# A two-layer graph attention kernel: three of every eight layer 0 tiles gathered by indirect DMAs

## The chip, the core and the metric

The kernel runs on one core of a Trainium2 chip. The metric is the device time of one execution in microseconds (us). The engines are PE (TensorE matmuls; PEld is its weight load), DVE (VectorE), ACT (ScalarE), POOL (GpSimd) and SP, which only issues DMAs here.

## The reference

16 graphs ("batches" below) of 1024 nodes with 64 features, and an int32 adjacency matrix of 1024 x 1024 each, symmetric, with about 0.8% of its entries set and the diagonal. Two layers, each followed by a residual and a layer norm:

```
# layer 0: 8 heads of 64, edges = adj (0 or 1 here)
q, k, v = heads(x @ Wq + bq), heads(x @ Wk + bk), heads(x @ Wv + bv)
scores  = leaky_relu(q . k / 8 + edge_bias[edges], 0.2), -1e9 where edges == 0
x = layernorm(x + softmax(scores) @ v @ Wp + bp)
# layer 1: one head, additive scores
hp = x @ lin_w.T + lin_b ; u, v = hp @ W1.T, hp @ W2.T
e  = a . leaky_relu(u_i + v_j, 0.2), -9e15 where adj == 0
x  = layernorm(x + elu(softmax(e) @ hp))
```

## The kernel before, in words

**Neighbour lists.** Since a node has only about nine neighbours, the kernel never forms 1024 x 1024 scores. Eight nodes share one list of neighbour slots: `SLOTS` = 120, of which 112 hold the union of the eight nodes' neighbours and 8 the nodes themselves. `prepare` (L308) makes the lists of a batch on DVE out of the adjacency matrix (matmuls `pat` L333, then rounds of MAX8 and MATCH_REPLACE8), as columns `col` that go to DRAM and as the mask of who is whose neighbour. It is a generator of 41 pieces (`PIECES` L255). `finish` (L423) makes the mask.

**Tiles.** A batch is 8 tiles of 128 nodes, that is 16 lists. A tile of either layer passes through these methods:

- `load` (L460): a DMA on SP brings the tile's list columns to all partitions (`cb`, 544 KB).
- `indicate` (L468): two DVE instructions (L475) compare `cb` with row numbers, which gives 0/1 matrices `f`.
- `gather` (L488), in two halves `hs`: 26 bf16 matmuls each (L499) multiply the batch's features, split by `thirds` (L445, POOL) into three bf16 parts, with `f`. So the neighbours' features arrive as columns (64 features on the partitions, slots along the row); ACT copies them out of PSUM (L505) into `xg`. `own` (L481, POOL, L484) adds the 8 own columns.
- `turn` (L509): 8 transposes (L518) make rows `xn` (slots on the partitions) of `xg`, and ACT copies them out (L519).
- Layer 0: `queries`, `score` (PE L603; DVE L611, L619, L620), `exps` (ACT L629), `divide` (DVE L636, POOL L637), `turn_weights` (PE L645), `attend` (PE L655), `heads` (PE L671, every second tile), `rows`, `residual`. Layer 1: `own_rows` (POOL L728), `project` (PE L740, L746; ACT L751; DVE L752), `weigh` (PE L766), `exps`, `turn_weights` (PE L780, DVE L782), `attend`, `rows`, `residual`.

**Order.** The loop at L883 is written out by hand, and every engine executes its instructions in the order of the program (`tc.manual_schedule`). Step `g` holds tile `g` of layer 0 (the later methods belong to tiles g-1 to g-3) and tile `g - LAG` of layer 1, 12 steps behind, so that eight steps do one batch of both layers. At five places in each step `lists.place` (L858) draws pieces: those of the next batch's `prepare`, as many as `QUOTA` says, and one of a list `side` (`finish`, and layer 1's `end`). At t = 6 the next batch's `Layer0` begins (L940: transposes `px`, then `thirds` in one block on POOL), at t = 2 the batch's `Layer1`. `Norm.scale` (L547) runs on POOL over a whole batch at once.

**Buffers.** In PSUM `ps_s` has two banks, which `score`, `heads` and `project` take in turn; `ps_g`, `ps_p` two each; in `ps_z` the tag "e" is one bank, shared by `back` (the rows of both layers), `weigh`'s scores and layer 1's `turn_weights`.

Of the kernel before, what the change touches and what calls it, by code (L numbers as in the profile page):

```python
# [9 lines left out]
F32 = mybir.dt.float32  # L10
# [12 lines left out]
GR = 8  # L23
# [10 lines left out]
def kernel(  # L34
# [204 lines left out]
    root = fst.tile([P, 1], F32, name="root")  # L239
    nc.vector.memset(root, -0.5)  # L240
    setup.close()

# [11 lines left out]
    KEPT = 40  # L254
    PIECES = 41  # L255
    MULT = 4
# [24 lines left out]

    started, edges, masks, late = {}, {}, {}, {}

    def start(b):

        xs = dbl.tile([P, NT, D], F32, tag="xs", bufs=3, name=f"xs_{b}")
        dg = sml.tile([P, NT], I32, tag="dg", bufs=2, name=f"dg_{b}")
        diag = adj[b].rearrange("r c -> (r c)")[0 : N * N : N + 1]
        for n in range(2):
            nc.sync.dma_start(xs[sub(n), :, :], by_rows(x[b], n))  # L290
            nc.sync.dma_start(
                dg[sub(n), :], diag[n * 512 : n * 512 + 512].rearrange("(t r) -> r t", r=D)
            )
        ads = {}

        def load(k):
            hs, T = divmod(k, NT)
            if hs < 2:
                ads[k] = dbl.tile([P, 2, SEG], I32, tag="ad", bufs=4, name=f"ad_{b}_{hs}_{T}")
                nc.sync.dma_start(  # L300
                    ads[k], adj[b, ts(T, P), :].rearrange("p (n c) -> p n c", n=2)[:, :, hs * SEG : hs * SEG + SEG]
                )

        for k in range(4):
            load(k)
        started[b] = xs, dg, ads, load

    def prepare(b):  # L308

        if b not in started:  # L310
            start(b)
        xs, dg, ads, load = started.pop(b)
        flags = sml.tile([P, 32], F32, tag="flags", bufs=2, name=f"flags_{b}")
# [95 lines left out]
        yield  # L409

        rows_s = per.tile([P, NT, 2 * CAP2], BF16, tag="rows_s", name=f"rows_s_{b}")
        for n in range(2):
            for q in range(NQ):
# [5 lines left out]
                )  # L419
        edges[b] = (xs, col_d)  # L420
        late[b] = (flags, dg, rows_s)

    def finish(b):  # L423

        flags, dg, rows_s = late.pop(b)
        mask = dbl.tile([P, NT, SLOTS], BF16, tag="mask", bufs=4, name=f"mask_{b}")
        nc.vector.tensor_scalar(mask[:, :, 0 : 2 * CAP2], rows_s, code, NEG, ALU.not_equal, ALU.mult)
# [17 lines left out]
    def thirds(src, tag, nm):  # L445

        t3 = dbl.tile([P, 3, NT, D], BF16, tag=tag, bufs=3, name=f"{tag}_{nm}")
        rest = src
        less = per.tile([P, NT, D], F32, tag="less", name=f"less_{tag}_{nm}")
        for k in range(3):  # L450
            nc.gpsimd.tensor_copy(t3[:, k, :, :], rest)
            if k < 2:
                nc.gpsimd.tensor_tensor(less, rest, t3[:, k, :, :], ALU.subtract)
                rest = less
        return t3

    class Tiles:


        def load(self, t):  # L460
            nm = f"{self.b}_{self.layer}_{t}"
            self.cb[t] = cb = dbl.tile([P, NSEG, 2, NQ, WIN], BF16, tag="cb", bufs=3, name=f"cb_{nm}")
            nc.sync.dma_start(
                cb.rearrange("p s n q k -> p (s n q k)"),
                self.col_d[t].rearrange("s n q k -> (s n q k)").unsqueeze(0).to_broadcast([P, NSEG * 2 * NQ * WIN]),
            )
# [54 lines left out]
        def begin(self, x_):  # L521

            b = self.b
            px = ps_g.tile([P, 512], F32, tag="g", name=f"px{self.layer}_{b}")
            columns_T(px, x_)
            self.xT = dbl.tile([P, 512], F32, tag=f"xT{self.layer}", name=f"xT{self.layer}_{b}")
            nc.scalar.copy(self.xT, px)
            self.t3 = thirds(x_, "x3", f"{self.layer}_{b}")
            self.f, self.xg, self.xn = {}, {}, {}

    def banks(tag, name):
# [3 lines left out]
    class Norm:  # L535
# [10 lines left out]

        def scale(self, dst, y):  # L547
            rs = sml.tile([P, NT], F32, tag="rs", name=f"rs_{self.nm}")
            nc.gpsimd.tensor_tensor(rs, self.mv[:, :, 1], eps.to_broadcast([P, NT]), ALU.add)
            nc.gpsimd.tensor_tensor(rs, rs, root.to_broadcast([P, NT]), ALU.pow)  # L550
            nc.gpsimd.tensor_tensor(dst, y, self.mv[:, :, 0:1].to_broadcast([P, NT, D]), ALU.subtract)
            nc.gpsimd.tensor_tensor(dst, dst, rs.unsqueeze(2).to_broadcast([P, NT, D]), ALU.mult)  # L552

    class Layer0(Tiles):
        layer = 0

        def __init__(self, b):
            self.b, self.cb, (self.xs, self.col_d) = b, {}, edges[b]
            self.begin(self.xs)
            self.mx = dbl.tile([P, 2, NG // 4], F32, tag="mx", name=f"mx_{b}")  # L560
            self.y = dbl.tile([P, NT, D], F32, tag="y", name=f"y0_{b}")
            self.norm = Norm(f"0_{b}")
            self.qp, self.ls, self.den, self.w = {}, {}, {}, {}

        def constants(self):
# [124 lines left out]
        def residual(self, t):  # L690
            if t % 2 == 0:
                return
            nc.vector.tensor_tensor(self.y[:, t - 1 : t + 1, :], self.pr, self.xs[:, t - 1 : t + 1, :], ALU.add)
            for t_ in (t - 1, t):
                self.norm.look(self.y, t_)

        def end(self):
            x1 = dbl.tile([P, NT, D], F32, tag="x1", name=f"x1_{self.b}")
            self.norm.scale(x1, self.y)

# [3 lines left out]
            nc.vector.tensor_tensor(bad, bad, low, ALU.max)  # L704
            return x1

    class Layer1(Tiles):
        layer = 1

        def __init__(self, b, x1):  # L710
            self.b, self.cb, self.x1, (_, self.col_d) = b, {}, x1, edges[b]
            self.begin(x1)
# [4 lines left out]
        def sums(self):  # L717
            pu = ps_g.tile([P, NT, D], F32, tag="g", name=f"pu_{self.b}")
            for t in range(NT):
                for n in range(2):  # L720
                    nc.tensor.matmul(pu[sub(n), t, :], self.xT[:, ts(t, D)], w1h[:, n, :], start=True, stop=True)
            self.u = dbl.tile([P, NT, D], F32, tag="u", name=f"u_{self.b}")
            nc.vector.tensor_tensor(self.u, pu, rows_b[:, 0:1, :].to_broadcast([P, NT, D]), ALU.add)
# [85 lines left out]
        def end(self):  # L809
# [12 lines left out]
            norm = Norm(f"1_{b}")  # L822
            for t in range(0, NT, 2):
                norm.look(y, t)
                norm.look(y, t + 1)
                yield
            norm.scale(o, y)
            yield
            for n in range(2):
# [7 lines left out]
    PLACES = 5  # L837
    QUOTA = (3, 3, 5, 6, 6, 6, 6, 6)
    l0, l1 = {}, {}
# [6 lines left out]
    class Lists:  # L846


        def __init__(self):
# [6 lines left out]
            self.done, self.part, self.side = 0, None, []  # L856

        def place(self, g, k):  # L858
            b, t = divmod(g + AHEAD, NT)
            due = PIECES * b + sum(QUOTA[:t]) + QUOTA[t] * (k + 1) // PLACES  # L860
            last = k == PLACES - 1
            while self.done < due and self.part != ("keys" if last else "sums"):
                self.part = next(self.work, None)
                self.done += 1
# [7 lines left out]
    with tc.manual_schedule(engines={getattr(mybir.EngineType, e) for e in order}):  # L872
        for _ in prepare(0):
            pass
        for _ in finish(0):
            pass
        l0[0] = Layer0(0)
        l0[0].constants()
        l0[0].load(0)
# [3 lines left out]
        for g in range(NT * B + LAG + 7):  # L883
            u = g - LAG
            b, t = divmod(g, NT)
            if t == 0 and 0 < b < B:
                lists.side.append(finish(b))
            lists.place(g, 0)
            at(l0, g - 2, "exps", 0, range(4))
            at(l0, g - 1, "score", lambda: at(l0, g - 2, "divide", 0))  # L890
            if (g - 1) // NT not in l0:
                at(l0, g - 2, "divide", 0)
            at(l0, g - 2, "exps", 1, range(2))
            at(l0, g, "gather", 0)
            at(l0, g - 3, "heads")
            at(l0, g, "gather", 1)
            at(l0, g - 2, "exps", 1, range(2, 4))
            back = ps_z.tile([P, 3, D], F32, tag="e", name=f"back_{g}") if g > 3 else None
            at(l1, u - 3, "rows", back)
            at(l0, g - 3, "rows", back)  # L900
            at(l0, g, "queries")
            at(l1, u - 3, "residual")
            at(l0, g - 3, "residual")
            if t == 6 and b - 2 in l1:
                lists.side.append(l1[b - 2].end())
            at(l0, g - 2, "divide", 1)
            at(l1, u - 1, "project")
            lists.place(g, 1)
            at(l1, u, "gather", 0)
            at(l0, g - 1, "turn")  # L910
            lists.place(g, 2)
            at(l1, u - 1, "weigh")
            at(l1, u - 1, "exps")
            at(l0, g + 1, "indicate")
            at(l0, g + 2, "load")
            at(l1, u, "gather", 1)
            if t == 2 and b - 1 in l0:
                x1 = l0[b - 1].end()
            at(l0, g - 2, "turn_weights")
            at(l1, u - 2, "turn_weights")  # L920
            at(l1, u - 1, "turn")
# [15 lines left out]
            if t == 3 and b - 1 in l1:  # L937
                l1[b - 1].sums()
            if t == NT - AHEAD and b + 1 < B:
                l0[b + 1] = Layer0(b + 1)  # L940
                l0[b + 1].load(0)
# [415 lines left out]
```

## Time and profile before

| | us |
|---|---|
| three runs, median | 2505.18 (2500.58 to 2507.12) |
| the profiled execution | 2508.74 |
| its span in the trace | 2506.8 |
| PE, DVE, ACT, POOL busy in it | 2308.1, 2012.1, 1445.2, 912.9 |
| first score of layer 0 (L603) | at 102.3 |
| eight steps of the middle (1366.9 to 1512.1) | 145.2 |
| last score of layer 0 | at 2354.1 |

The page of a profile gives busy times over the whole span. For a kernel of repeated steps the windows view is of more use: it cuts the trace at the start of each step's score and gives each engine's busy time between the cuts. The waits view says who waited for whom, and the timeline shows instructions in order. A window in the tables below is one step of the loop; t is its number in the batch, 0 to 7.

### The profile page before, as it was taken

The numbers are of one execution on the slowest core, as the hardware profiler recorded it, in microseconds if no ns is written. First come the engines' busy times: TensorE is split into PE (matmuls) and PEld (weight loads), VectorE is DVE, ScalarE is ACT, GpSimd is POOL, SyncE is SP. The second block draws the span as 40 slices with busy tenths as digits, with TensorE's granted clock in tenths as the row PEclk, the third lists the DMA queues.
The fourth block names the chain that finished last, engine by engine and source line by source line (L and its number), as shares of the span: only waits on it lengthen the run. The fifth ranks groups of instructions, "written<-read, shape, count | busy, mean of one in ns | idle before, by whom it ended". The sixth has DMA issues, their size and how long they took to land. (4 is left out here: it accounts for less than half of the span.)

```text
span 2506.8 us, 110853 instructions
## 1 busy us (share of the span) xinstructions
PE 2308.1 (92%) x48706; PEld 1957.7 (78%) x48706; DVE 2012.1 (80%) x5237; ACT 1445.2 (58%) x4401; POOL 912.9 (36%) x1106
## 2 busy tenths in 40 slices
PE   5387999999999999999999999999999999999986
PEld 3376788878788887878788787888878888888864
DVE  6687879888888988888898888889888888876642
ACT  0154656656565665656566566656656665666743
POOL 1133333434334343433434343342434434243331
PEclk9998999999999999999999999999999999999998
DMA  3412332423233242323324232332423233221210
GB/s 102 122 59 89 104 103 78 133 77 116 73 102 108 78 133 80 114 73 107 103 78 133 84 109 75 106 103 78 133 86 108 81 100 106 62 92 57 66 52 18
DMA packets 190543, 230.66 MB, mean 92 GB/s; under 512 B 91492, under 2 KB 157092, under 8 KB 190052
## 3 DMA queue, kind: packets, MB, share of 16 engines
q1 hardware_dynamic: 190052, 223.49, 28.3%
q8 instruction: 384, 6.29, 1.0%
q14 instruction: 107, 0.88, 0.1%
HBM read 218.23 MB, written 5.21 MB: 89 GB/s over the span
## 5 line engine op out<-in xcount | busy, mean ns | idle before, releaser
L499 PE MATMUL pg<-f,x 128*64 128x272 bf16 (+2 forms) x13312 | 804.5, 272 | 37.4 <-DVE f L475 34.5
L499 PEld LDWEIGHTS <-x 128*64 128x64 bf16 x13312 | 662.0, 109 | 115.5 <-issue 70.4
L637 POOL TENSOR_TENSOR ls<-ls,den 128x480 f32<-128x480 f32 x256 | 285.8, 1117 | 921.1 <-DVE den L636 912.6
L475 DVE TENSOR_SCALAR f<-cb,jrow 128x2176 bf16<-128x2176 bf16 x512 | 491.6, 1001 | 0.3 <-DMA cb<-col_d 0.3
L505 ACT COPY xg<-pg 128x448 f32<-128x448 f32 x512 | 271.5, 530 | 356.1 <-PE pg L499 355.1
L629 ACT ACTIVATE ls<-ls,mx 128x120 f32<-128x120 f32 x1024 | 391.2, 386 | 4.8 <-DVE mx L620 4.8
L519 ACT COPY xn<-pt 120x512 f32<-120x512 f32 x512 | 277.3, 597 | 11.8 <-PE pt L518 7.1
L751 ACT ACTIVATE r<-pz 128x480 f32<-128x480 f32 x256 | 132.1, 568 | 247.0 <-PE pz L746 247.0
L518 PE MATMUL pt<-ident,xg 128*120 128x128 f32 x2048 | 273.9, 276 | 0.0
L484 POOL COPY xg<-xT 128x64 f32<-128x64 f32 x256 | 107.2, 426 | 387.9 <-PE pt L518 345.4
L518 PEld LDWEIGHTS pt<-ident,xg 128*120 128x120 f32 x2048 | 224.0, 137 | 27.3 <-issue 24.8
L752 DVE SCALAR_TENSOR_TENSOR r<-pz,r 128x480 f32<-128x480 f32 x256 | 155.4, 649 | 50.6 <-ACT r L751 50.6
L629 ACT ACTIVATION_READ_ACCUMULATOR ls<-ls,mx 128x1 f32 x1024 | 194.8, 190 | 0.0
L619 DVE SCALAR_TENSOR_TENSOR ls<-sc 128x480 f32<-128x480 f32 x256 | 191.5, 748 | 0.0
L620 DVE TENSOR_REDUCE mx<-ls 128x4 f32<-128x480 f32 x256 | 167.2, 653 | 8.8
L611 DVE TENSOR_TENSOR sc<-s,rowc 128x480 f32<-128x480 f32 x256 | 155.1, 647 | 22.7 <-PE s L603 21.0
L746 PEld LDWEIGHTS pz<-rw,ub 64*64 64x64 f32 x4096 | 122.6, 133 | 63.9 <-issue 58.5
L655 PE MATMUL z<-w,xn 120*64 120x64 f32 x4096 | 159.2, 227 | 4.4 <-ACT w L647 4.4
L587 DVE TENSOR_TENSOR qp<-pq,qb 128x512 f32<-128x512 f32 x128 | 87.9, 686 | 90.0 <-PE pq L586 89.8
L655 PEld LDWEIGHTS z<-w,xn 120*64 120x64 f32 x4096 | 138.4, 139 | 27.7 <-ACT w L647 19.4
L645 PE MATMUL pp<-ident,ls 128*120 128x128 f32 x1024 | 142.0, 280 | 19.3 <-POOL ls L637 16.6
L740 PE MATMUL pz<-xg,w2d 64*64 64x480 f32 x1024 | 140.4, 588 | 17.1 <-DVE sc L611 17.1
(212 smaller groups left out, 3881.1 us busy)
## 6 DMA issues: line engine op xcount, KB each, us to landing
cb<-col_d SPq DMA_DIRECT2D x256, 544.0 KB
ad<-in_adj_dram SPq DMA_DIRECT2D x256, 256.0 KB
xs<-in_x_dram SPq DMA_DIRECT2D x32, 128.0 KB
rows_s<-slot_d SPq DMA_DIRECT2D x256, 14.0 KB
out_dram<-o SPq DMA_DIRECT2D x32, 128.0 KB
col_d<-col SPq DMA_DIRECT2D x128, 4.2 KB
dg<-in_adj_dram SPq DMA_DIRECT2D x32, 2.0 KB
slot_d<-slot SPq DMA_DIRECT2D x16, 28.0 KB
```

What stands on the lines that cost most here:

```text
L475: nc.vector.tensor_scalar(fj.rearrange("p s n q k -> p (s n q k)"), cb.rearrange("p s n q k -> p (s n q k)"), jrow[:, j : j + 1], None, AL ...
L499: nc.tensor.matmul(pg[sub(n), :, FIRST * a_ + lo : FIRST * a_ + to], self.t3[:, k, 4 * hs + 2 * a_ + j, :], f[j][:, 2 * hs + a_, n, :, lo:to],
L505: nc.scalar.copy(dst, pg)
L518: nc.tensor.transpose(pt[:, q, :], xg[:, 4 * m + q, :], ident)
L519: nc.scalar.copy(self.xn[t][:, ts(m, 4), :], pt)
L611: nc.vector.tensor_tensor(sc, both[n], self.rowc[:, n, ts_].unsqueeze(2).to_broadcast([P, 4, SLOTS]), ALU.add)
L619: nc.vector.scalar_tensor_tensor(ls, scs[n], SLOPE, scs[n], ALU.mult, ALU.max)
L620: nc.vector.tensor_reduce(self.mx[:, n, ts_], ls, XX, ALU.max, negate=True)
L629: nc.scalar.activation(ls[:, q, :], ls[:, q, :], AF.Exp, bias=neg[:, q : q + 1], accum_out=den[:, q : q + 1])
L637: nc.gpsimd.tensor_tensor(ls, ls, den.unsqueeze(2).to_broadcast([P, 4, SLOTS]), ALU.mult)
L655: nc.tensor.matmul(zz[sub(n), q, :], xn[:, q, sub(n)], w_[n][:, q // 2, sub(q % 2)], start=True, stop=True)
L752: nc.vector.scalar_tensor_tensor(r, pz[n], SLOPE / (1.0 - SLOPE), r, ALU.mult, ALU.add)
```

## The change

- `start` also copies the batch's `x` into a DRAM `table` of 1025 rows, of which row 0 is a filler (three DMAs on SP). `prepare` makes, beside `col`, the 120 row numbers of every list (`tb`, `at_s`: six DVE instructions), one PE transpose and one DVE instruction bring them to `at_d` (lists along the row, slots on the partitions). It has 43 pieces now.
- `FETCHED = (2, 5, 7)`: for these layer 0 tiles `load`, `indicate` and `own` do nothing. `fetch` issues, from POOL, one indirect DMA for each of a tile's 16 lists: 120 rows of 64 f32, straight into the layout of `xn`. `Lists.fetches` spreads the 48 of a batch over the 40 places of eight steps, ahead of the other work of a place, two steps ahead of the tile that is being worked on. `gather` of such a tile is 8 transposes of `xn` into `xg` with two ACT copies; `turn` does nothing.
- In a fetched tile's step the order is another: both halves of the gather first, `queries` ahead of `heads`, and `turn` of the tile before earlier.
- Layer 1's `turn_weights` goes from behind `weigh` and the second half of layer 1's gather to a place ahead of them.
- `place` draws at most two pieces (except at the last place of a round of eight steps). `thirds` becomes five pieces on the side list; the next batch's `Layer0` begins at t = 4 and not 6. `Norm.scale` works on two tiles at a time, in place in layer 0. `u` and layer 1's `xT` have one buffer and not two, `mask` three and not four.

```diff
-    PIECES = 41
+    PIECES = 43
...
+            nc.sync.dma_start(
+                table[1 : N + 1, :].rearrange("(t n r) d -> n t r d", n=2, r=D)[n],
+                x[b, n * 512 : n * 512 + 512, :].rearrange("(t r) d -> t r d", r=D),
+            )
...
+    def fetch(b, t, k):
+        _, table, rows_at = edges[b]
+        if k == 0:
+            fetched[b, t] = dbl.tile([SLOTS, NQ, P], F32, tag="xf", bufs=3, name=f"xf_{b}_{t}")
+        n, q = divmod(k, NQ)
+        g = D * n + NQ * t + q
+        nc.gpsimd.indirect_dma_start(
+            out=fetched[b, t][:, q, sub(n)], out_offset=None, in_=table[:, :],
+            in_offset=bass.IndirectOffsetOnAxis(ap=rows_at[:, g : g + 1], axis=0),
+        )
...
+        def gather(self, t, hs):
+            if t not in FETCHED:
+                return super().gather(t, hs)
...
+            for q in range(4):
+                nc.tensor.transpose(pt[:, q, :], self.xn[t][:, 4 * hs + q, :], ident[0:SLOTS, 0:SLOTS])
+            nc.scalar.copy(self.xg[t][:, ts(hs, 4), :], pt)
...
-    QUOTA = (3, 3, 5, 6, 6, 6, 6, 6)
+    QUOTA = (3, 3, 5, 6, 6, 6, 7, 7)
+    FETCHED = (2, 5, 7)
...
+            end = self.done + 2 if (t, k) != (NT - 1, PLACES - 1) else due
...
+            if t in FETCHED:
+                at(l0, g, "gather", 0)
+                at(l0, g, "gather", 1)
+                at(l0, g - 2, "exps", 1, range(2))
+                at(l1, u - 3, "rows", back)
+                at(l0, g, "queries")
+                at(l0, g - 3, "heads")
...
             at(l1, u, "gather", 0)
-            at(l0, g - 1, "turn")
+            at(l1, u - 2, "turn_weights")
+            if t not in FETCHED:
+                at(l0, g - 1, "turn")
...
             at(l0, g - 2, "turn_weights")
-            at(l1, u - 2, "turn_weights")
             at(l1, u - 1, "turn")
```

## The prediction, written before the changed kernel was run

> **What bounds the kernel now.** I read the page first, then the windows of one batch, then the timeline of a step, then who waited for whom. The page's first line:
>
> ```profile
> PE 2308.1 (92%) x48706; PEld 1957.7 (78%) x48706; DVE 2012.1 (80%) x5237; ACT 1445.2 (58%) x4401; POOL 912.9 (36%) x1106
> ```
>
> PE leads and DVE is near, but an average over the span does not say which of them ends a step. The windows, cut at each step's score (t = 0 to 7), do. Columns: length, then busy us of PE, PEld, DVE, ACT, POOL with counts, granted clock, DMA share, GB/s.
>
> ```profile
> 1366.90:1384.30 17.40, 17.40 (x347) 14.41 (x346) 12.24 (x26) 12.56 (x43) 6.31 (x9) 1.00 0.56 183
> 1384.30:1404.80 20.50, 18.81 (x414) 16.06 (x413) 18.01 (x51) 9.79 (x28) 10.42 (x12) 1.00 0.09 32
> 1404.80:1423.90 19.10, 17.45 (x374) 15.05 (x373) 18.64 (x45) 12.00 (x39) 6.00 (x8) 1.00 0.24 70
> 1423.90:1442.30 18.40, 17.67 (x381) 14.86 (x379) 15.88 (x43) 10.57 (x31) 3.77 (x5) 1.00 0.41 126
> 1442.30:1457.90 15.60, 15.60 (x344) 13.73 (x341) 13.31 (x32) 10.87 (x33) 3.84 (x5) 1.00 0.13 39
> 1457.90:1475.80 17.90, 17.90 (x415) 15.60 (x413) 14.51 (x36) 12.02 (x37) 5.32 (x6) 1.00 0.29 74
> 1475.80:1494.50 18.70, 18.48 (x411) 15.37 (x409) 17.08 (x44) 12.59 (x43) 16.34 (x20) 1.00 0.60 201
> 1494.50:1512.10 17.60, 17.45 (x378) 14.87 (x377) 15.14 (x42) 9.58 (x27) 4.58 (x5) 1.00 0.21 66
> sum 145.20, PE 140.75 PEld 119.94 DVE 124.80 ACT 89.99 POOL 56.59; mean PE 17.59 PEld 14.99 DVE 15.60 ACT 11.25 POOL 7.07
> ```
>
> Steps 0, 4 and 5 are PE from end to end. PE is idle for 4.5 us a batch, nearly all at t = 1 to 3, where DVE is at its fullest. The waits of PE in these 145.2 us agree; all of the larger ones are DVE's:
>
> ```profile
> PE po L671 <- DVE sc L611: 1.5, 2, 1.0
> PE pz L740 <- DVE sc L611: 0.8, 1, 0.8
> PE e L766 <- DVE r L752: 0.7, 2, 0.5
> ```
>
> So PE sets the end of a batch, DVE is behind it with 86% of the time, and POOL has 88.6 us to spare.
>
> **What goes from PE.** The timeline at t = 0 (start, duration):
>
> ```profile
> 1368.12 2.99 PE L499 MATMUL pg<-f,x 128*64 128x272 bf16 x52
> 1370.93 0.28 PE L280 MATMUL back<-lin,aT 128*64 128x64 f32 x4
> ...
> 1379.56 1.04 PE L518 MATMUL pt<-ident,xg 128*120 128x128 f32 x8
> 1380.52 1.15 PE L655 MATMUL z<-w,xn 120*64 120x64 f32 x32
> ```
>
> From its start to the next group's start a layer 0 gather holds PE for 2.81 us, a `turn` for 0.96 us. A fetched tile loses both and gains eight transposes of `xn`, which have 120 columns and not 128, so at most the same 0.96. That is 3 x 2.81 = 8.4 us less per batch; the transpose for `at_d` adds the 0.11 us from L780's start (1379.45) to the next. Net 8.3 of 145.2, and 136.9 if PE's idle time stayed at 4.5.
>
> **DVE.** Six `indicate` instructions fewer at 1.0 us (L475's mean on the page) are -6.0. Added per batch: six small ones on 128 x 136 or fewer elements and one of 120 x 128. The like rows are 0.30 (L393), 0.23 (L390), 0.17 (L401 to L403) and 0.29 (L782): about 1.7 us. Net -4.3, or 120.5. It is ill placed, though: the indicates go at t = 1, 4 and 6 (one step ahead of their tile), PE's gathers at t = 2, 5 and 7. At t = 2 DVE still has its 18.6 us, against 17.45 - 2.8 = 14.6 on PE. That tile's gain will largely turn into waiting for DVE. In return t = 1 (DVE 18.0 in 20.5) gets air, and two pieces per place at most keep long runs of list work from standing ahead of a score in DVE's queue. I take PE's idle time as 6.0 in place of 4.5; from 2.5 (the cap and the earlier layer 1 transpose end half the waits) to 10.5 (t = 2 and t = 0 wholly DVE's) are the ends.
>
> **POOL.** No row shows an indirect DMA. Nearest rows: 0.43 us for L484's copy of 128 x 64, as many values as a fetch brings; 1.12 and 1.14 for the half-row products; 1.86 for the slowest, the power:
>
> ```profile
> L637 POOL TENSOR_TENSOR ls<-ls,den 128x480 f32<-128x480 f32 x256 | 285.8, 1117 | 921.1 <-DVE den L636 912.6
> L484 POOL COPY xg<-xT 128x64 f32<-128x64 f32 x256 | 107.2, 426 | 387.9 <-PE pt L518 345.4
> ```
>
> Ends 0.43 and 1.86; I take 1.15, their middle and L637's size. 48 fetches are 20.6, **55.2** or 89.3 us per batch. `Norm.scale` in pairs is 8 x (0.2 + a power of two columns, by a quarter of 1.86 about 0.47, + two of 128 columns at about 0.45) = 12.6 for 2 x 4.4 before, +3.8; three own copies fewer, -1.2. POOL comes to 56.6 + 2.6 + 55.2 = 114 of some 138. In front of every `divide` (L637) there now stands a fetch or two. Their cover is the time from `divide` to `turn_weights`, some 6 us of project, gather, turn and weigh at t = 0. A backlog of four fetches would use it up. The thirds' block at t = 6, which made POOL 16.3 of 18.7, is spread out; unspread it would not fit beside six fetches (6.9 us) there.
>
> [...]
>
> **The rest.** ACT: four copies of 0.53 to 0.60 go and two of that size come per tile, on an engine with 55 us free. SP: three `cb` issues fewer, three for `table` more; DMA's share is 0.60 at most. `px` (1.05 us on PE) moves from t = 6 to t = 4. The first fetch of a batch waits for `at_d`; behind it on POOL stands tile 4's `divide`. One buffer for `u` makes DVE's L723 at t = 3 wait for POOL's last L728 of the batch before; behind it stand the next places' list pieces and, a step on, the scores. It costs what POOL is late, 0 to 1 us, and lies in the 6.0. At the start 12 fetches (13.8 us) and then `thirds` (4.2) follow `at_d`, which can't be there before DVE ends the lists at 76.7. So the first gather comes near 96 and not at 93.6: +3. In the tail the last normalisation is shorter by some 3. They cancel.
>
> **The sum.** 145.2 - 8.3 + 1.5 = 138.4 a batch, 6.8 less. Fifteen batches run this way (344.7 us onwards at full width, the second nearly so): -102. In the first batch, whose eight steps take 103.5 us with PE far from full, six indicates less save 3 and seven new instructions take 1 to 2: nothing. The profiled execution of 2508.7 (span 2506.8) becomes 2407; it lay 3.6 above the median of the runs, so against that median the forecast is **2403**. With 2.5 or 10.5 of idle time it is 2350 or 2470.
>
> **Rivals.**
> - *DVE takes the place of PE.* POOL goes from 39% to about 83% busy, so more of the 26 remaining indicates run beside it. If all took 1.37 us like the pair at 1405, DVE would gain 26 x 0.37 = 9.6 and stand at 130; at t = 2 and 0 nothing would hide it. I price it at 5 us a batch: 2478. For it: L475 from 772 to 1798 ns. Against it: those two ran beside products of 512 columns, and no row shows an indirect DMA beside L475.
> - *POOL becomes the bound, slower than before.* POOL needs 59.2 + 48 c. It passes my 138.4 at c = 1.65 and today's 145.2 at c = 1.79 us per fetch. At the upper end, 1.86, a batch is 148.5: +3.3 x 15 and some 5 at the start, 2560. For it: the row of 1.86 for only 8 columns. Against it: all other rows with as many values are far below.
> - *It doesn't do what it says.* The order within the fetched steps turns the freed 2.8 us into waits of PE for ACT's copies of `xg` behind four exps: no change, 2505. Against it: PE has queries and rows (1.3 us) in between.
>
> **Chances.** Forecast 0.60 (its own range 2350 to 2470), DVE 0.12, POOL 0.21, no change 0.05, other 0.02. Faster by over 0.3% (about what a measurement of this kernel can tell from no change) 0.72, within it 0.05, slower 0.23. The range 2350 to 2560 leaves out some 0.07 below and 0.10 above.
>
> **What would show it.** L499 down to 10,816 matmuls and near 650 us; windows of 15 to 16 us at t = 5 and 7 and hardly shorter ones at t = 2; fetches near 1.15 us on POOL, and POOL near 114 of 138. I am wrong if POOL is full in every window, if PE waits for `pp` on POOL's `ls`, if L475's mean passes 1.2 us, or if PE's idle time per batch is over 12 us.

## The result, and the profile after

The changed kernel takes **2906.8 us** (median of 4 runs, 2900.1 to 2924.0) against 2504.8 before: 1.162 times the time, 95% interval 1.160 to 1.164. The forecast was 2403, and 2350 to 2560 the range. It is slower by 402 us, and no rival had a price near that.

The page of the changed kernel (span 2902.4 us). First the engines' busy time, then the granted clock of PE in 40 slices, then two groups: the fetch and the indicator rows:

```profile
PE 2454.6 (85%) x46226; PEld 1999.0 (69%) x46226; DVE 1980.5 (68%) x5261; ACT 1395.4 (48%) x4305; POOL 1760.5 (61%) x2213
...
PEclk9877889999989989999999999999998889989998
...
L615 POOL DMA_INDIRECT xf<-table,at_d x768 | 815.9, 1062 | 220.9 <-issue 180.7
...
L519 DVE TENSOR_SCALAR f<-cb,jrow 128x2176 bf16<-128x2176 bf16 x416 | 383.4, 963 | 0.0
```

PE has 2480 matmuls fewer and is yet busy for 146 us more. POOL, from which the fetches were expected to take most, is at 61% and is not the bound. A fetch costs it 1.06 us, and 0.24 us of idle time stand ahead of each (180.7 us over some 740 of them).

The windows of one batch in the middle, cut at each step's score (t = 0 to 7), in the columns of the table before:

```profile
1603.50:1623.60 20.10, 18.22 (x349) 14.89 (x348) 12.44 (x24) 10.73 (x33) 15.35 (x19) 1.00 0.62 189
1623.60:1646.90 23.30, 18.79 (x368) 15.05 (x368) 19.89 (x64) 11.70 (x36) 13.84 (x17) 1.00 0.18 47
1646.90:1664.70 17.80, 17.62 (x362) 15.11 (x361) 13.63 (x31) 10.86 (x36) 10.36 (x11) 0.90 0.54 141
1664.70:1691.20 26.50, 22.26 (x411) 18.59 (x409) 17.34 (x48) 10.76 (x33) 16.34 (x20) 0.88 0.15 37
1691.20:1710.00 18.80, 15.02 (x297) 12.49 (x297) 16.32 (x36) 10.93 (x33) 12.40 (x14) 0.95 0.09 12
1710.00:1730.40 20.40, 19.11 (x373) 16.09 (x372) 13.62 (x32) 11.01 (x34) 11.11 (x15) 0.86 0.39 103
1730.40:1753.40 23.00, 19.80 (x366) 14.77 (x365) 13.24 (x37) 13.19 (x46) 20.41 (x30) 0.93 0.56 176
1753.40:1772.70 19.30, 16.87 (x370) 14.30 (x370) 16.27 (x46) 7.81 (x20) 10.35 (x15) 1.00 0.05 10
sum 169.20, PE 147.68 PEld 121.27 DVE 122.74 ACT 86.99 POOL 110.17; mean PE 18.46 PEld 15.16 DVE 15.34 ACT 10.87 POOL 13.77
```

A batch takes 169.2 us, 24 more than before. PE is idle for 21.5 of them (169.20 - 147.68), not for 4.5. It is also busy for 147.7 and not for the 132.5 that three gathers fewer should leave. The clock column says a part of why: it was 1.00 in all eight windows before, and falls to between 0.86 and 0.95 in five of them now. DVE (122.7) and POOL (110.2) are where the prediction put them (120.5 and 114). So the amount of work on these two engines is not the loss; PE itself has become slow.

What PE waited for, over the whole run:

```profile
PE z L752 <- ACT w L744: 67.3, 109, 2.2
PE pi L457 <- DVE at_s L443: 45.9, 13, 22.6
PE e L860 <- DVE eT L876: 45.6, 65, 1.9
PE px L290 <- issue: 31.6, 93, 0.5
PE prc L669 <- issue: 30.7, 53, 2.5
...
PE s L700 <- issue: 24.9, 61, 1.3
```

Three of the six say "issue": PE waited for nothing that the profile shows. Summed over all lines, such idle time of over 60 ns is 124 us here and was 5 us before. No wait of this kind stood in the prediction, so the experiments look for its cause.

### The profile page after: what moved, and what is told of

It reads as the page before. It is cut to its first block, busy times and chain, and to the rows that moved or that the text cites. A ratio compares the mean times of both kernels' runs of the same rounds, so it can differ in the third digit from the quotient of the medians.

```text
span 2902.4 us, 106586 instructions
## 1 busy us (share of the span) xinstructions
PE 2454.6 (85%) x46226; PEld 1999.0 (69%) x46226; DVE 1980.5 (68%) x5261; ACT 1395.4 (48%) x4305; POOL 1760.5 (61%) x2213
## 4 chain that ended last, share of the span: by engine, by line
PE 65%; DVE 21%; issue 5%; ACT 5%; another core or an unknown queue 1%; DMA 1%; POOL 1%; SPq 0%; POOLq 0%; ACTq 0%; DVEq 0%
PE pg L543 15%; PE s L700 7%; PE pt L562 6%; DVE f L519 4%; PE pq L683 4%; PE z L752 4%; PE pz L834 4%; PE pp L742 4%; PE pa L885 4%; PE pz L840 3%; DVE r L846 3%; PE e L860 3%; PE po L768 3%; PE pat L356 3%; PE px L290 2%
## 5 line engine op out<-in xcount | busy, mean ns | idle before, releaser
L615 POOL DMA_INDIRECT xf<-table,at_d x768 | 815.9, 1062 | 220.9 <-issue 180.7
L543 PE MATMUL pg<-f,x 128*64 128x272 bf16 (+2 forms) x10816 | 698.6, 281 | 9.7 <-issue 7.2
L543 PEld LDWEIGHTS <-x 128*64 128x64 bf16 x10816 | 558.5, 113 | 96.8 <-issue 54.6
L549 ACT COPY xg<-pg 128x448 f32<-128x448 f32 x416 | 220.9, 532 | 500.0 <-PE pg L543 396.5
L519 DVE TENSOR_SCALAR f<-cb,jrow 128x2176 bf16<-128x2176 bf16 x416 | 383.4, 963 | 0.0
L562 PE MATMUL pt<-ident,xg 128*120 128x128 f32 x1664 | 225.7, 277 | 27.0 <-ACT xg L549 26.7
L563 ACT COPY xn<-pt 120x512 f32<-120x512 f32 x416 | 226.3, 601 | 39.1 <-PE pt L562 34.5
L562 PEld LDWEIGHTS pt<-ident,xg 128*120 128x120 f32 x1664 | 185.5, 139 | 39.9 <-ACT xg L549 31.8
L752 PEld LDWEIGHTS z<-w,xn 120*64 120x64 f32 x2560 | 99.5, 142 | 111.7 <-ACT w L744 87.4
L885 PE MATMUL pa<-eT,xn 120*64 120x8 f32 x4096 | 162.1, 209 | 4.1 <-ACT xn L563 2.8
```

Of the source, the lines that this page charges most:

```text
L519: nc.vector.tensor_scalar(fj.rearrange("p s n q k -> p (s n q k)"), cb.rearrange("p s n q k -> p (s n q k)"), jrow[:, j : j + 1], None, AL ...
L543: nc.tensor.matmul(pg[sub(n), :, FIRST * a_ + lo : FIRST * a_ + to], self.t3[:, k, 4 * hs + 2 * a_ + j, :], f[j][:, 2 * hs + a_, n, :, lo:to],
L549: nc.scalar.copy(dst, pg)
L562: nc.tensor.transpose(pt[:, q, :], xg[:, 4 * m + q, :], ident)
L563: nc.scalar.copy(self.xn[t][:, ts(m, 4), :], pt)
L615: nc.gpsimd.indirect_dma_start(out=fetched[b, t][:, q, sub(n)], out_offset=None, in_=table[:, :], in_offset=bass.IndirectOffsetOnAxis(ap=r ...
```

## The experiments

**A. Which part of the change costs the time.** Three kernels take the change apart. The first has all the edits but no fetched tile:

```diff
-    FETCHED = (2, 5, 7)
+    FETCHED = ()
```

> The changed kernel with an empty list of fetched tiles: no indirect DMA, every layer 0 tile gathered by matmuls in the old order; the capped pieces, the spread thirds, the pairwise normalisation, the early layer 1 transpose and the row numbers' transpose stay. Theory A (the indirect DMAs on POOL cost the time, through waits of PE and the clock that falls after them): about the time before, 2480 to 2530 us, and few 'issue' gaps on PE. Theory B (the order around the fetches - the early layer 1 transpose, the pieces, less matmul work between dependent steps - costs it): well above, 2600 us or more.

Measured: 2528.1 us, 1.010 [1.007, 1.013] times the kernel before. All that the change does besides fetching (the list of rows, the table, the capped pieces, `Norm.scale` in pairs, the thirds in pieces, the early transpose) costs 25 us by itself.

The second issues all 768 fetches and uses none of them (every tile is gathered by PE, in the old order):

```diff
+    USED = ()
...
-            if t not in FETCHED:
+            if t not in USED:
```

> All 768 indirect DMAs are issued as in the changed kernel, but nothing reads what they bring: every layer 0 tile is gathered by matmuls in the old order. Theory A: 2750 us or more, with the 'issue' gaps of PE in px and prc and half-clock stretches as in the changed kernel. Theory B: within 60 us of the kernel without fetched tiles.

Measured: 2924.1 us, 1.168 [1.161, 1.175]. **The fetches alone add 396 us**, though nobody waits for one. The idle time of PE on issue is 136 us.

The third is the reverse: the order and the savings of the change, but no DMA. The fetched tiles are a tile of zeros that lies ready:

```diff
-        nc.gpsimd.indirect_dma_start(
...
+            fetched[b, t] = still
```

> The changed kernel with its order and its transposes of fetched tiles, but without the indirect DMAs: the fetched tiles are read from one constant tile of zeros, so the neighbours' features of tiles 2, 5 and 7 are left out of the computation. Theory A: what the prediction's sum gives, 2380 to 2420 us. Theory B: 2800 us or more, because the waits for eT, w and xg remain without any DMA.

Measured: 2462.5 us, 0.984 [0.981, 0.987]. Even fetches that cost nothing would have brought 41 us and not 102. In a batch in its middle, cut at the scores as before, PE's work is what was forecast (shown are t = 2, 3 and 7 and the sum):

```profile
1390.10:1406.20 16.10, 15.79 (x366) 13.87 (x365) 15.69 (x41) 10.82 (x37) 8.47 (x9) 1.00 0.60 167
1406.20:1426.70 20.50, 18.47 (x414) 15.81 (x413) 16.80 (x48) 10.67 (x32) 5.68 (x9) 1.00 0.10 34
...
1476.80:1495.20 18.40, 16.61 (x374) 14.09 (x373) 15.85 (x46) 8.63 (x25) 8.05 (x14) 1.00 0.07 21
sum 140.70, PE 132.66 PEld 111.87 DVE 117.85 ACT 86.56 POOL 62.80; mean PE 16.58 PEld 13.98 DVE 14.73 ACT 10.82 POOL 7.85
```

PE is busy 8.1 us less than before (140.75), against a forecast of 8.3, and idle for 8.0 us, against a forecast of 6.0 within 2.5 to 10.5. The steps are not the ones that were forecast: t = 2, which was to be hardly shorter, falls from 19.1 to 16.1 us, while t = 3 grows from 18.4 to 20.5 and t = 7 from 17.6 to 18.4. Over the third to the fifteenth batch the gain is 4.0 us each (141.7 for 145.7). The start gives some of it back: the first score comes at 107.5 us for 102.3, and the first two batches take 252 us for 242.

The early transpose was tried by itself, put back behind the second half of the gather in the changed kernel:

```diff
-            at(l1, u - 2, "turn_weights")
             at(l0, g + 1, "indicate")
...
             at(l0, g - 2, "turn_weights")
+            at(l1, u - 2, "turn_weights")
```

> The changed kernel with layer 1's transpose of its weights back behind layer 0's, as before; all else as changed. If the early transpose costs what PE waits for eT before the scores (45.6 us in the trace) and half as much again by the clock: 2830 to 2860 us. If it is of no account: 2890 to 2920 us.

Measured: 2805.9 us, 1.121 [1.114, 1.127], so the early place costs about 101 us in the changed kernel. The same edit in the kernel without DMAs and in the one without fetched tiles:

> The free fetch (no DMA; the fetched tiles are read from a tile of zeros, so the output is not the reference's) with layer 1's transpose of its weights back in its old place behind the gather. Free fetches with the early transpose gave 2462.5 us, 41 under the kernel before, where the gathers taken away are worth 102. Theory 1: PE waits at the early transposes for the second exps and for w (z from ACT w 41 us there) and moving them back gives most of the missing 61: 2405 to 2430 us. Theory 2: the order is not to blame, the remaining 61 are other edits (Norm in pairs, thirds in pieces, the turn behind queries) and the clock: 2450 to 2475 us.

> No tile fetched, all other edits in, but layer 1's transpose of its weights back in its old place. With it early, the same kernel took 2528.1, 25 over the kernel before. Theory 1 (the early transpose costs by itself): 2500 to 2510 us. Theory 2 (the 25 us are the other edits, the list of rows, the table, Norm in pairs): 2520 to 2530 us.

Measured: 2493.0 us (0.996 [0.994, 0.998]) and 2508.8 us (1.002 [1.001, 1.003]). With free fetches the early place is better by 30 us, a sign that neither theory of the first text had. Without fetched tiles it is worse by 19, and that is most of the 25 us above (theory 1 of the second text). So the early transpose isn't good or bad by itself; what decides it is not shown by these runs.

**B. What it is about a fetch.** All kernels from here on are the second one (fetches issued, nothing used; 2924 us), with the instruction replaced; they stand against the 2528 us without fetches. First POOL's time without a DMA, a memset of about a fetch's length:

```diff
-        nc.gpsimd.indirect_dma_start(
...
+        nc.gpsimd.memset(idle, 0.0)
```

> The kernel whose fetches nobody reads (2924 us; without fetches 2528), with a memset of 128 x 1120 f32 on POOL (about 1.04 us by the setup's row of 0.95 us for 1024) in the place of each of the 768 indirect DMAs: POOL is as busy, no DMA. If what costs is that POOL's own products stand behind the fetches: 2850 us or more. If it is the DMAs: 2520 to 2600 us, without 'issue' gaps of PE at the score.

Measured: 2800.8 us, 1.118 [1.112, 1.124], so +273. By the time alone, two thirds of the loss would be POOL's occupancy. The pages contradict that; the kernel with memsets, then the one with fetches:

```profile
L614 POOL MEMSET idle<- 128x1120 f32 x768 | 882.2, 1149 | 19.6
...
L519 DVE TENSOR_SCALAR f<-cb,jrow 128x2176 bf16<-128x2176 bf16 x512 | 582.6, 1181 | 0.5 <-DMA cb<-col_d 0.5
```

```profile
L615 POOL DMA_INDIRECT xf<-table,at_d x768 | 818.1, 1065 | 207.5 <-issue 182.1
...
L519 DVE TENSOR_SCALAR f<-cb,jrow 128x2176 bf16<-128x2176 bf16 x512 | 438.3, 899 | 8.1 <-PE pt L562 7.3
```

The memsets lengthen DVE's indicator rows to 1.18 us (0.85 without fetches), DVE is busy for 2300 us, and half the chain that ended last is DVE's. PE's idle time on issue is 4 us. The memset makes a loss of its own, by DVE; it doesn't stand for the full fetch, which leaves the row at 0.90 and DVE busy for 2012 us. The experiment was ill chosen.

Then the same bytes without POOL, and with POOL (`nc.gpsimd.dma_start`) but without indices:

```diff
-        nc.gpsimd.indirect_dma_start(
...
+        nc.sync.dma_start(fetched[b, t][:, q, sub(n)], table[8 * g : 8 * g + SLOTS, :] if g < 100 else table[0:SLOTS, :])
```

> The same kernel with 768 plain DMAs of the same 120 rows of 256 bytes from the table, issued on SP in place of POOL's indirect ones. If the traffic of small rows costs: 2850 us or more. If the issuing on POOL costs: 2530 to 2620 us (some 0.5 us of SP's queue each, 23 us of a batch, ahead of the cb loads).

> The same kernel with 768 plain DMAs of 120 rows of 256 bytes issued on POOL: the same bytes by POOL's queue, without the list of row numbers. If a DMA's issue on POOL costs whatever it fetches: 2850 us or more. If only the indirect form does: under 2650 us.

Measured: 2534.6 us (1.012 [1.006, 1.017]) from SP, +7, and 2575.5 us (1.028 [1.021, 1.035]) from POOL, +47. The traffic is as good as free, though these DMAs read 120 consecutive rows and not scattered ones. A plain DMA holds POOL for 0.62 us.

Then the size of an indirect fetch, by its rows and by the length of a row:

```diff
-            out=fetched[b, t][:, q, sub(n)], out_offset=None, in_=table[:, :],
-            in_offset=bass.IndirectOffsetOnAxis(ap=rows_at[:, g : g + 1], axis=0),
+            out=fetched[b, t][0:16, q, sub(n)], out_offset=None, in_=table[:, :],
+            in_offset=bass.IndirectOffsetOnAxis(ap=rows_at[0:16, g : g + 1], axis=0),
```

> The same kernel with indirect DMAs of 16 rows in place of 120. If the cost goes with the number of DMAs: 2800 us or more. If it goes with the rows: the extra time over 2528 is a seventh, about 2580 us. POOL's instruction: near 1.06 us still if its time is fixed, near 0.3 us if it goes by rows.

> The fetches issued and not used, with 64 rows each in place of 120 (the kernel without fetches 2528; 16 rows 2613; 120 rows 2924). POOL's time for one should stay near 1.0 us, as with 16 rows (0.96) and 120 rows (1.06). Theory 1: PE's instructions are held up while the descriptors of an indirect DMA are made, by the row: a line through 16 and 120 rows gives 2757 us (2700 to 2810), and PE's idle time put down to issue, 2.6 us with 16 rows and 136 with 120, lies near 65. Theory 2: it is POOL's occupancy alone: as with 16 rows, 2600 to 2640. Theory 3: something overflows between 64 and 120 rows: also near 2613, or near 2924 if it overflows below 64.

> The fetches issued and not used, 96 rows of 256 bytes each (16 rows 2613 us, 64 rows 2611, 120 rows 2924; 120 rows of 32 bytes 2633). If the holding up of PE grows with the bytes beyond those of 64 rows, a line from 64 to 120 rows gives 2790 (2720 to 2850), with 70 to 100 us of PE idle on issue; if it is a limit that only 120 rows exceed, 2600 to 2640; if a limit between 64 and 96 rows sets it, 2880 to 2940.

The same edit with 64 and with 96. For shorter rows the table is read as rows of 8 or 32 values:

```diff
-            out=fetched[b, t][:, q, sub(n)], out_offset=None, in_=table[:, :],
+            out=fetched[b, t][:, q, D * n : D * n + 8], out_offset=None,
+            in_=table.rearrange("r (a d) -> (r a) d", d=8),
```

> The fetches issued and not used, 120 rows each but of 32 bytes in place of 256, so that the bytes are those of the 16-row kernel (2613 us) and the number of indices that of the 120-row one (2924). Theory 1: the number of indices counts: 2890 to 2950 us, and PE idle on issue 110 to 160 us. Theory 2: the bytes count: 2600 to 2640 us, and issue under 10 us.

> The fetches issued and not used, 120 rows of 128 bytes each, so 15 KB, about the bytes of 64 rows of 256 (2611 us), with the indices of the full fetch (2924). If the bytes of one fetch decide, 2610 to 2650 us and issue under 20 us; if the number of rows decides once they are longer than 32 bytes, 2850 to 2940; if both count by a product, between, about 2750.

| rows x bytes | KB | us | over 2528 | POOL us each | PE idle on issue, us |
|---|---|---|---|---|---|
| 16 x 256 | 4 | 2613.3 | 85 | 0.96 | 3 |
| 64 x 256 | 16 | 2611.5 | 83 | 1.01 | 19 |
| 96 x 256 | 24 | 2609.9 | 82 | 1.03 | 18 |
| 120 x 32 | 4 | 2633.5 | 105 | 1.07 | 7 |
| 120 x 128 | 15 | 2639.3 | 111 | 1.07 | 9 |
| 120 x 256 | 30 | 2924.1 | 396 | 1.06 | 136 |

(The last row is the second kernel of part A. POOL's times are the means on the pages.) This refutes a price per row, per byte or per us of POOL for the large step: POOL's time hardly changes. The smaller fetches cost 82 to 111 us (the plain DMAs of POOL 47). On top of it, only the full fetch makes PE slow, by about 290 us more. With rows of 256 bytes there is a jump between 24 KB (82 us) and 30 KB (396 us), not a slope.

Two things come with the 82 to 111 us: POOL is held for a microsecond 768 times, and DVE's own instructions last longer. The engines and one group of DVE without fetches, then with 96 rows:

```profile
PE 2308.7 (91%) x48722; PEld 1957.1 (77%) x48722; DVE 1973.3 (78%) x5357; ACT 1447.6 (57%) x4401; POOL 1015.2 (40%) x1493
...
L716 DVE SCALAR_TENSOR_TENSOR ls<-sc 128x480 f32<-128x480 f32 x256 | 175.6, 686 | 0.0
```

```profile
PE 2336.3 (90%) x48722; PEld 1973.4 (76%) x48722; DVE 2063.1 (79%) x5357; ACT 1446.9 (56%) x4401; POOL 1750.8 (67%) x2261
...
L716 DVE SCALAR_TENSOR_TENSOR ls<-sc 128x480 f32<-128x480 f32 x256 | 207.4, 810 | 0.0
```

The same 5357 instructions of DVE take 90 us more here, and 88 to 107 us more with the other four small fetches. It is 62 us with the plain DMAs of POOL. What PE loses, it may lose to POOL's lateness or to DVE's, and no run separates the two. The large step is not DVE's: with full fetches DVE is busy for only 39 us more than without fetches.

The waits of PE with full fetches, then with 96 rows (the only entry on issue among its largest):

```profile
PE s L700 <- issue: 55.9, 160, 0.5
...
PE prc L669 <- issue: 20.7, 37, 3.4
PE pg L543 <- issue: 18.1, 59, 1.0
```

```profile
PE pi L457 <- issue: 10.7, 11, 1.0
```

How such a stretch looks. In the kernel with full fetches, three windows within a step, in the columns of the windows above:

```profile
1318.60:1320.60 2.00, 2.00 (x72) 1.93 (x70) 1.97 (x3) 1.70 (x9) 1.81 (x2) 1.00 0.94 277
1320.60:1322.85 2.25, 1.13 (x17) 0.46 (x6) 1.31 (x5) 1.21 (x7) 1.94 (x3) 1.00 0.59 127
1322.85:1323.10 0.25, 0.24 (x8) 0.24 (x12) 0.06 (x1) 0.00 (x0) 0.10 (x1) 1.00 0.82 171
```

And its timeline there (start, duration, idle time before in brackets):

```profile
1319.73 1.30 POOL L615 DMA_INDIRECT xf<-table,at_d  x1 [0.19 <-issue]
1320.19 0.82 PE L700 MATMUL s<-xg,qp 64*64 64x120 f32 x17
...
1321.31 0.36 PE L700 MATMUL s<-xg,qp 64*64 64x120 f32 x2 [0.31 <-issue]
1321.34 0.99 POOL L615 DMA_INDIRECT xf<-table,at_d  x1 [0.30 <-issue]
...
1322.10 0.36 PE L700 MATMUL s<-xg,qp 64*64 64x120 f32 x2 [0.43 <-issue]
...
1322.86 0.38 PE L700 MATMUL s<-xg,qp 64*64 64x120 f32 x4 [0.40 <-issue]
```

The 48 matmuls of a score depend on nothing that is late: 18 of them have run in 0.82 us (the line counts 17, since its window begins at 1320.50). Then PE starts two at 1321.31, two at 1322.10 and the next at 1322.86, waiting for nothing that the profile shows in between, at full clock. Two fetches stand on POOL in this stretch, and neither ACT nor DVE has idle time put down to issue in it. Over the whole run, 133 of the 136 us of such idle time end within 1.8 us of the start of a fetch, which is 42% of the run. PE's instructions coming late would be another cause, but the loads of the queue that the profile calls "instruction" are the same 384 and take no longer (1.08 us on average, 1.10 without fetches).

Since the second kernel runs the same 48,722 matmuls in the same order as the one without fetches, the time from each start to the next can be subtracted. PE's run is 386 us longer by that. **312 of them lie between the start of a fetch on POOL and 0.6 us after its end**, a part of the time that is 40% of the run. With 96 rows the same sum is 59 of 75, so it is the amount that differs and not the share. Against 16 rows the lines that lose most are the score (131 us), the turn (43), the gather (40), `prc` (30) and `px` (28): mostly groups of short f32 matmuls, of which PE starts many per us (18 in 0.82 us of the score above).

**C. Whether that is the loss of the changed kernel.** The changed kernel's order, tiles of zeros as in the third kernel, and fetches that nobody reads: first with rows of 32 bytes, then the full ones:

```diff
             fetched[b, t] = still
+            xf[b, t] = dbl.tile([SLOTS, NQ, P], F32, tag="xf", bufs=2, name=f"xf_{b}_{t}")
+        nc.gpsimd.indirect_dma_start(
...
```

> The changed kernel with fetches of 120 rows of 32 bytes, which hold POOL as long (1.07 us) and PE hardly, and with the fetched tiles read from a tile of zeros (the output is not the reference's). Without any DMA this order took 2462. If POOL's occupancy adds here what it added in the old order (2633 - 2528 = 105): 2567 (2540 to 2590). If the new order is more exposed to POOL's lateness than the old one: 2620 to 2700.

> The changed kernel, with all its fetches of 120 rows of 256 bytes issued, but the fetched tiles read from a tile of zeros (the output is not the reference's), so that no transpose waits for a transfer. With rows of 32 bytes it took 2593, 314 less than the changed kernel. If the loss lies in the issue and the size of the fetches: 2870 to 2910 us. If PE's waiting for the fetched rows has a part in it, lower by that part, at most the 23 us by which 314 exceeds the 291 of the old order.

Measured: 2593.1 us (1.035 [1.031, 1.040]) and 2884.0 us (1.152 [1.149, 1.156]). With the third kernel and the changed one this is a chain in which, from the second row on, each link changes one thing (the last link also gives the fetched tiles three buffers and not two):

| | us | step |
|---|---|---|
| before | 2504.8 | |
| changed order, fetches free | 2462.5 | -42 |
| + fetches of 120 x 32 bytes | 2593.1 | +131 |
| + rows of 256 bytes: PE slow to issue | 2884.0 | +291 |
| + the transposes read what was fetched | 2906.8 | +23 |

(The -42 is against the median of all runs of before; the 41 above is against those taken with that kernel.) The +291 is what the old order showed (396 less 105). The +131 is a little more than the 105 of the old order; here too DVE is busy for longer, 2003.4 us for 1907.6 in the kernel with free fetches. A batch of the kernel with narrow fetches, its steps t = 3 to 5 and its sum:

```profile
1483.80:1506.00 22.20, 20.19 (x417) 17.16 (x413) 17.30 (x45) 10.77 (x33) 15.21 (x20) 0.92 0.14 34
1506.00:1525.10 19.10, 16.24 (x300) 13.69 (x298) 17.48 (x36) 11.92 (x39) 15.13 (x17) 0.88 0.09 8
1525.10:1543.90 18.80, 18.80 (x370) 15.98 (x370) 13.06 (x32) 9.87 (x30) 9.47 (x12) 0.85 0.36 97
...
sum 151.30, PE 138.97 PEld 116.97 DVE 123.43 ACT 86.68 POOL 109.14; mean PE 17.37 PEld 14.62 DVE 15.43 ACT 10.83 POOL 13.64
```

Against free fetches (140.70, PE 132.66) PE is idle for 4.3 us more, and busy for 6.3 us more with the same matmuls. With them comes a lower granted clock: 0.92, 0.88 and 0.85 in the three steps shown, 1.00 in all of them with free fetches. As an estimate from these three shares and the lengths of the steps, 6.9 us at full clock are lacking, which covers the 6.3. So the smaller fetches are paid twice, as a wait and as a slower PE. The clock records of the kernels before and after have two values alone, 1.00 and 0.50 (half clock below). In the trace with narrow fetches more idle time stands ahead of half clock than elsewhere: of the 8 us ahead of a half-clock stretch, PE was idle for 2.5 on average (39 stretches, the first 110 us left out), and for 0.8 of any 8 us. Over the whole run PE is at half clock for 64 us before, 132 with free fetches, 267 with narrow ones, 421 with full ones (the kernel of 2884.0 us) and 458 in the changed kernel.

The old place of layer 1's transpose in this kernel:

> As the kernel with fetches of 32-byte rows and tiles of zeros, but with layer 1's transpose of its weights back in its old place. Without DMAs the old place is worse by 30 us (2493 against 2462), with the full fetches it is better by 100 (2806 against 2907). If POOL's lateness by occupancy makes the early transposes wait (the weights pass POOL's divide), the old place is better here too: 20 to 80 us under the kernel with the early one. If only PE's being held up does, it stays worse by about 30.

Measured: 2608.0 us (1.041 [1.034, 1.048]), 15 us over the early place. By the two intervals that can be told neither from nothing nor from 30, but a gain of 20 to 80 is excluded: what the smaller fetches do to POOL and DVE isn't what makes the early transpose a loss. It is worse by 101 us only with the full fetches, where PE is slow to issue. By which wait that comes about was not separated.

Last, a mend that computes the same values: a fetch takes only the 112 rows of the lists (28 KB), and the 8 own rows, which lie one behind the other, come by a plain DMA:

```diff
+        if q == 0:
+            first = n * 512 + t * D
+            nc.sync.dma_start(
+                fetched[b, t][2 * CAP2 : SLOTS, :, sub(n)],
+                x[b, first : first + D, :].rearrange("(q j) d -> j q d", j=GR),
+            )
...
-            in_offset=bass.IndirectOffsetOnAxis(ap=rows_at[:, g : g + 1], axis=0),
+            in_offset=bass.IndirectOffsetOnAxis(ap=rows_at[0 : 2 * CAP2, g : g + 1], axis=0),
```

> The changed kernel with the rows of each fetch cut from 120 to the 112 of the lists; the 8 own rows of each group, which lie one behind the other, come by one plain DMA of SP for 8 groups. The fetches of 96 rows of 256 bytes cost 82 us over the kernel without them, those of 120 rows 396. If the limit lies above 112 rows, PE's idle time on issue falls from 124 us to under 25 and the time to that of the kernel with narrow fetches (2593) plus the 192 plain DMAs: 2590 to 2650. If it lies between 96 and 112, the time stays at 2880 to 2920.

Measured: 2883.4 us (1.152 [1.146, 1.158]), PE idle on issue 133 us. 112 rows of 256 bytes show the large step too; with 96 rows, in the old order (2609.9 us, 18 us on issue), it was not there. The 23 us gained are no cure.

No version with fetches that was tried beats the kernel before: even fetches of 120 x 32 bytes, with 7 us of idle time on issue in part B, cost 131 us, where the changed order with free fetches brings 42.

## Why the prediction was wrong, step by step

**The step that failed is the price of a fetch.** The prediction counted a fetch as POOL's own time, free to the kernel short of "a backlog of four fetches", and put its effect on PE at nothing. With POOL's time as forecast, the runs show +131 us for the smaller fetches and +291 us more for 120 rows of 256 bytes, with which PE becomes slow to issue.

**PE's saving was right.** 8.3 us per batch forecast, 8.1 measured with free fetches. The gathers' matmuls are 10,816, as said. They were put near 650 us; they take 665.0 with free fetches and 698.6 in the changed kernel, where PE issues slowly (124 us idle on issue) and is at half clock for longer (458 us for 132).

**DVE's sum was right, its rows were not.** 120.5 us forecast, 117.9 with free fetches, 123.4 with narrow ones and 122.7 after. The rival "DVE takes the place of PE" looked at the indicator rows. Its 1.37 us are half of this line of the timeline before, a pair that ran beside POOL's work for `thirds`; the row's median in that batch was 0.78 us:

```profile
1405.08 2.73 DVE L475 TENSOR_SCALAR f<-cb,jrow 128x2176 bf16<-128x2176 bf16 x2
```

Over the run the rows' mean went down, from 1.00 to 0.96 us (0.85 without fetches). But the smaller fetches lengthen other rows (part B), so a part of that rival came; how large a part of the 131 us stays open. On POOL a fetch takes 0.98 to 1.47 us, median 1.02.

**POOL's sum was right, its consequence wrong.** A fetch was put at 1.15 us and is 1.06, plus 0.24 of idle time ahead of it. The power of two columns was put at 0.47 and is 0.81 us. POOL stands at 110 us per batch (114 forecast), and at 61% it isn't the bound. That the rival "POOL becomes the bound" has a price (2560) near the 2593 of the narrow fetches is luck, since its reason is wrong. The narrow fetches cost 131 us with POOL at 67%. It shows hardly as a wait for POOL: PE's waits for layer 1's `eT`, which DVE writes, rise from 40 to 72 us and those for the weights, which ACT writes, from 41 to 58, while those on POOL's `ls` go from 23 to 31.

**PE's idle time was too low.** 6.0 us per batch with ends 2.5 and 10.5: within them with free fetches (8.0, though not in the steps that were named), 12.3 with narrow ones, 21.5 after. My own sign of error, "PE's idle time per batch is over 12 us", is what came.

**The clock was left out.** The prediction took PE's durations from windows at full clock. Half clock rose together with the idle time: 132, 267 and 458 us over the run with free fetches, narrow ones and in the changed kernel, with 8.0, 12.3 and 21.5 us of idle time per batch. The changed kernel is at half clock for 394 us more than the kernel before (64 us); as an estimate from that, at most 197 of the 402 us are the clock's.

**The first batch was not "nothing".** (Its six `indicate` instructions fewer were put at 3 us there and at 6.0 in the sum for DVE.) The first score comes 9.7 us later (3 forecast), and the first two batches take 313.5 us for 242.4, of which free fetches explain 10.

**The large step could not be read from the trace of before:** that with indirect fetches of 28 or 30 KB (112 or 120 rows of 256 bytes) PE is slow to issue, +291 us of 402 for 30 KB. No row of before shows an indirect DMA. I bounded its cost by POOL's rows alone and, the rival on DVE's indicator rows aside, gave no end to what it might do to another engine. The upper end, 2560, came from POOL as the bound; nothing in the working stood for a loss on PE itself.

## What to carry to other kernels

Count an operation that the trace doesn't show as a risk for every engine and not only for the one that runs it, and try it alone, issued and not used, before building on it: that one run here gave +396 us. Where PE sets the pace, a third of free time on a helper is not yet room for new work: here 768 small fetches on POOL cost 82 to 131 us, and in the new order, with 131 us of that, PE was at half clock for 267 us and not 132. When an experiment stands in for a cost, look whether it brings one of its own, as the memset did.

## What the runs showed of the hardware

- **PE issues slowly with indirect DMAs of 112 or 120 rows of 256 bytes on POOL.** Its idle time on issue is 118 to 136 us in the five kernels with such fetches, against 3 to 19 with the smaller ones of part B's table and 5 in the kernel before. Of the 136 us in the kernel whose fetches nobody reads, 133 end within 1.8 us of the start of a fetch. Plain DMAs of 120 consecutive rows cost 47 us in all from POOL and 7 from SP, not 396. With nothing waiting for the data and nearly the same time on POOL (1.06 and 1.03 us), the same matmuls took 314 us longer with 120 rows than with 96 (2924.1 and 2609.9). What in the chip it is stays open, and full fetches spaced far apart were not tried.
- An indirect DMA holds POOL for 0.96 us with 16 rows and 1.06 with 120, so it hardly grows with the rows. A plain one of 120 rows holds it for 0.62.
- A memset of 128 x 1120 on POOL takes 1.15 us and lengthens DVE's `tensor_scalar` of 2176 bf16 values from 0.85 to 1.18 us on average. The smaller fetches leave that row at 0.87 to 0.91 but lengthen others: the cast `ab<-ad` takes 0.64 to 0.74 us (0.54 with free fetches, in the changed order), `ls<-sc` 0.75 to 0.85 in place of 0.69.
- A power of 2 columns takes POOL 0.81 us, of 8 columns 1.86: by a line through the two, 0.46 us and 0.175 a column.
